# One product and a VectorE transpose for each squaring of a spectral-norm chain

## The chip, the cores and the metric

The kernel runs on one core of a Trainium2 chip. The metric is the device time of one execution in microseconds, the median of several runs.

## The reference

Four layers follow one another on x of shape (8, 512, 32, 32). Only the first is touched by the change.

```python
# layer 0
f_x = relu(batchnorm(conv1x1(x, Wf, bf), gamma_f, beta_f)).reshape(b, 64, hw)
g_x = relu(batchnorm(conv1x1(x, Wg, bg), gamma_g, beta_g)).reshape(b, 64, hw)
h_x = conv1x1(x, Wh, bh).reshape(b, 64, hw)
z = einsum('bcn,bcm->bnm', f_x, g_x)                 # hw x hw, rank 64
sigma = svd(z, compute_uv=False)[:, 0][:, None, None]
z2 = einsum('bnm,bcm->bcn', z / sigma, h_x).reshape(b, 64, h, w)
x = conv1x1(z2, Wv, bv) + x
# layer 1: group norm, attention over the 1024 positions, x + proj
# layer 2: attention with 128 channels, folded batch norm, + x
# layer 3: sign(x + bias) times sign(W), batch norm, + x, PReLU
```

## The kernel before

The images are in pairs, one on partitions 0-63 and one on 64-127. The largest singular value of an image comes from two 64x64 Gram matrices, F = f f' and G = g g': the largest eigenvalue of F G is sigma squared. `gram(j, i, ...)` makes them for pair j by TensorE and stores them, masked to the two diagonal 64x64 blocks (`mask2`, L1351), in `gm[j]`, 128x128 each: F at index 0, G at 1 and g h' at 2.

`chain(j, split)` then takes the product and squares it again and again. F G is not symmetric, and a product on TensorE takes its left operand transposed, so the chain keeps the matrix and its transpose: `products` makes both (L1029 and L1030, each 128 columns), and `evict` copies both from PSUM into `cur` (128 x 2 x 128). There are 21 products' steps in a chain: the first, then seven rounds (`NSTEP + 1`) of three squarings, the last round of two. In each third step the matrix is scaled by its trace: `diagonal` multiplies by the identity and sums each row (L1056), `total` sums the rows by a product with `mask2` (L1060) and copies the sum to `tr` (L1061), a reciprocal follows (L1083), and the eviction scales. These are the scaled steps, the others are plain. Logarithms of the traces give 1/sigma at the end, which scales g h' into index 0 of `gm[j]` (L1112), from where `weights0` (L290) takes it.

With `split`, in the head, the two products have banks of their own and VectorE and ScalarE evict one each. Without it both lie in one bank and one instruction evicts them: ScalarE in a plain step (L1043), VectorE in a scaled one (L1051).

The order of the work:
- The head. The first pair's chain (`jl`) runs alone, before any attention can start. TensorE's order there is the program's (`tc.manual_schedule`). Beside each step of the chain, `next(todo)` puts a piece of other work, a filler: 16 pieces of the weight product `wu` and of the first pair's last Gram, then 26 pieces of the other pairs' transposes, Grams and bias rows (L1142, L1342, L1313, L1315, L1420), then 16 of the weight product `wo` (L1288). A piece of a weight product is one product of 512 columns.
- `entering(0)`/`enter` of the first image follows, with the fillers left over between its steps. For each 512-column block it adds the layer's result to x (L421) and takes statistics (L424), then makes the group-norm means.
- The main part, one image after another in `fast`: seven-product matrix multiplications (`seven`, L388, whose results VectorE takes up at L345), attention values (L557), then layers 2 and 3. The other three pairs' chains are hidden there: `chore(2)` takes one step of `behind` for every second step of the image's own work. Outside the head the order on each engine is made by a scheduler from the dependencies.

The head's fillers before:

```python
for k, _ in enumerate(chain(jl, True)):
    for _ in range(4 if k == 3 * NSTEP + 3 else 2 if k % 3 == 1 or k == 0 else 1):
        next(todo, None)
...
for n in (2, 3, 3, 3, 4, 4, 6):
    next(steps)
    for _ in range(n):
        next(todo, None)
```

The functions that the diff touches, and what calls them:

Of the kernel before, what the change touches and what calls it, by code (L numbers as in the profile page):

```python
# [8 lines left out]
F32 = mybir.dt.float32  # L9
F16 = mybir.dt.float16  # L10
I32 = mybir.dt.int32
AF = mybir.ActivationFunctionType
ALU = mybir.AluOpType
# [3 lines left out]
P = 128  # L17
# [8 lines left out]
MID = 64  # L26
NPAIR = B // 2
# [42 lines left out]
NSTEP = 6  # L70
# [15 lines left out]
def kernel(  # L86
# [17 lines left out]
    nc = tc.nc  # L104
    mm = nc.tensor.matmul

    const = ctx.enter_context(tc.tile_pool(name="const", bufs=1))
    wpool = ctx.enter_context(tc.tile_pool(name="weights", bufs=1))
    keep = ctx.enter_context(tc.tile_pool(name="keep", bufs=1))
    xpool = ctx.enter_context(tc.tile_pool(name="x", bufs=2))  # L110
    stat = ctx.enter_context(tc.tile_pool(name="stat", bufs=2))
    spin = ctx.enter_context(tc.tile_pool(name="spin", bufs=2))
# [10 lines left out]
    def bank():  # L123
        return psum["bank"].tile([P, HF], F32, tag="bank", name="bank")
# [20 lines left out]
    def side(i):  # L145

        return slice(i * MID, (i + 1) * MID)
# [21 lines left out]
    ident = const.tile([P, P], F32, tag="ident", name="ident")  # L169
    make_identity(nc, ident)  # L170

    def block_ones(size, value, name):

        n = P // size
        member = const.tile([P, n], F32, tag=name + "_m", name=name + "_m")
        nc.vector.tensor_reduce(
            member, ident.rearrange("p (g j) -> p g j", j=size), AX.X, ALU.add
        )
        t = const.tile([P, n, size], F32, tag=name, name=name)
        nc.vector.tensor_scalar(  # L180
            t, member.unsqueeze(2).to_broadcast([P, n, size]), value, None, ALU.mult
        )
        return t.rearrange("p g j -> p (g j)")

    mask2 = block_ones(MID, 1.0, "mask2")
    gmat = block_ones(GROUP, 1.0 / GROUP, "gmat")

    fold = a1.tile([P, 2, MID], F32, tag="fold", name="fold")
# [13 lines left out]
    wv2 = const.tile([P, C], F32, tag="wv2", name="wv2")  # L202
# [40 lines left out]

    r_dram = [dram.tile([4, N // 4], F32, name=f"r_dram{i}") for i in range(2 * B)]
    f_dram = [dram.tile([P, HF], F32, name=f"f_dram{b}") for b in range(B)]
    gm = [keep.tile([P, 3, P], F32, tag=f"gm{j}", name=f"gm{j}") for j in range(NPAIR)]
    sw3 = wpool.tile([P, CC, C // 2], F16, tag="sw3", name="sw3")
    round3 = const.tile([P, 1], F32, tag="round3", name="round3")
    nc.gpsimd.memset(round3, ROUND)
# [36 lines left out]
    def weights0(b):  # L286

        rr = side(b % 2)
        ps = bank()
        mm(out=ps, lhsT=gm[b // 2][rr, 0, :], rhs=wv2[rr, :], start=True, stop=True)  # L290
        t = fpool.tile([P, C], F32, tag="pv", name="pv", bufs=2)
        if b % 2:
            nc.vector.tensor_copy(t, ps)
        else:
            nc.scalar.copy(t, ps)
        return t
# [716 lines left out]

        return hb, got[0] if more else None

    def chain(j, split):

        ff, gg, gh = (gm[j][:, i, :] for i in range(3))  # L1020
        tr = spin.tile([P, NSTEP + 3], F32, tag="tr", name="tr")

        def column(name):
            return spin.tile([P, 1], F32, tag=name, name=name)

        def products(a, at):
            ps = [bank()] if not split else [bank(), bank()]
            pa, pb = ps[0][:, 0:P], ps[-1][:, 0:P] if split else ps[0][:, P : 2 * P]
            mm(out=pa, lhsT=at, rhs=a, start=True, stop=True)  # L1029
            mm(out=pb, lhsT=a, rhs=at, start=True, stop=True)  # L1030
            return ps[0], pa, pb

        def evict(got, r=None, again=None, full=None):

            both, pa, pb = got
            cur = spin.tile([P, 2, P], F32, tag="cur", name="cur")
            parts = [(cur[:, 0], pa), (cur[:, 1], pb)]
            if not split:
                parts = [(cur.rearrange("p i c -> p (i c)"), both[:, 0 : 2 * P])]
            for i, (dst, ps) in enumerate(parts):  # L1040
                if r is None:
                    if i or not split:
                        nc.scalar.copy(dst, ps)  # L1043
                    else:
                        nc.vector.tensor_copy(dst, ps)
                elif i:
                    nc.scalar.activation(dst, ps, AF.Copy, scale=full)
                elif again is None:
                    nc.vector.tensor_scalar(dst, ps, r, None, ALU.mult)
                else:  # L1050
                    nc.vector.tensor_scalar(dst, ps, r, again, ALU.mult, ALU.mult)  # L1051
            return cur

        def diagonal(u, v, t):
            d = spin.tile([P, P], F32, tag="diag", name="diag", bufs=1)
            nc.vector.scalar_tensor_tensor(d, u, 1.0, v, ALU.mult, ALU.mult, accum_out=t)  # L1056

        def total(t, s, n=1):
            ps = bank()
            mm(out=ps[:, 0:n], lhsT=mask2, rhs=t, start=True, stop=True)  # L1060
            nc.vector.tensor_copy(tr[:, s : s + n], ps[:, 0:n])  # L1061

        t = column("tj")
        diagonal(ff, gg, t)
        got = products(gg, ff)
        total(t, 0)
        r = column("r")
        nc.vector.reciprocal(r, tr[:, 0:1])
        cur = evict(got, r, None, r)
        yield  # L1070

        root, half_ = column("root"), column("half_")
        nc.gpsimd.tensor_tensor(root, tr[:, 0:1], minus_half[:, 0:1], ALU.pow)
        nc.vector.tensor_tensor(half_, root, root, ALU.mult)
        nc.vector.tensor_tensor(half_, half_, tr[:, 0:1], ALU.mult)
        nc.vector.tensor_scalar(half_, half_, -0.5, 1.5, ALU.mult, ALU.add)
        nc.vector.tensor_tensor(root, root, half_, ALU.mult)
        for s in range(NSTEP + 1):
            got = products(cur[:, 0], cur[:, 1])
            if s:  # L1080
                total(t, s)
                r = column("r")
                nc.vector.reciprocal(r, tr[:, s : s + 1])  # L1083
                if split:
                    r2 = column("r2")
                    nc.vector.tensor_tensor(r2, r, r, ALU.mult)
                cur = evict(got, r, r, r2 if split else None)
            else:
                cur = evict(got)
            yield  # L1090
            for more in range(2 if s < NSTEP else 1):
                got = products(cur[:, 0], cur[:, 1])
                cur = evict(got)
                if more:
                    t = column("tj")
                    diagonal(got[1], ident, t)
                yield
        t = spin.tile([P, 2], F32, tag="td", name="td")
        diagonal(cur[:, 0], ident, t[:, 0:1])
        diagonal(cur[:, 0], cur[:, 1], t[:, 1:2])  # L1100
        total(t, NSTEP + 1, 2)

        ln = spin.tile([P, NSTEP + 2], F32, tag="ln", name="ln")
        rsig = column("rsig")
        nc.scalar.activation(ln, tr[:, 1:], AF.Ln)
        nc.vector.tensor_tensor(ln, ln, shares, ALU.mult)
        nc.vector.tensor_reduce(rsig, ln, AX.X, ALU.add)
        nc.scalar.activation(rsig, rsig, AF.Exp, scale=-0.5)
        nc.vector.tensor_tensor(rsig, rsig, root, ALU.mult)
        for i in range(2):  # L1110
            rr = side(i)
            nc.vector.tensor_scalar(  # L1112
                ff[rr, :].rearrange("p (i c) -> p i c", c=MID),
                gh[rr, rr].unsqueeze(1).to_broadcast([MID, 2, MID]),
                rsig[rr, :],
                None,
                ALU.mult,
            )
        ready.add(j)
        yield  # L1120

# [2 lines left out]

    def chains():
        for j in rest:
            yield from chain(j, False)

    behind = chains()
    env = {}  # L1130
# [208 lines left out]
    def gram(j, i, lt, rhs):  # L1339
        ps = wide()  # L1340
        for t in range(NT):
            mm(  # L1342
                out=ps[:, 0:P],
                lhsT=lt[:, t, :],
                rhs=rhs[:, t, :],
                start=t == 0,
                stop=t == NT - 1,
            )
            if t == NT // 2 - 1:
                yield  # L1350
        nc.vector.tensor_tensor(gm[j][:, i, :], ps[:, 0:P], mask2, ALU.mult)  # L1351
        yield

    def turned_pair(j):
# [28 lines left out]
    ps = bank()  # L1383
# [5 lines left out]
    ps = bank()  # L1389
# [64 lines left out]
    relus = iter([(2 * j + k, i) for j in rest for i in range(2) for k in range(2)])  # L1454
    with tc.manual_schedule(engines={mybir.EngineType.PE}):
        steps = entering(0)
        for k, _ in enumerate(chain(jl, True)):

            for _ in range(4 if k == 3 * NSTEP + 3 else 2 if k % 3 == 1 or k == 0 else 1):
                next(todo, None)  # L1460
            for args in (next(relus, None),):
                if args:
                    relu(*args)
        for n in (2, 3, 3, 3, 4, 4, 6):
            next(steps)
            for _ in range(n):
                next(todo, None)
        for _ in todo:
            pass
# [195 lines left out]
```

## Time and profile before

| | |
|---|---|
| median of 3 runs | 1898.42 us (1897.82 to 1898.85) |
| span of the profiled execution | 1896.9 us |
| TensorE busy | 1878.3 us (99%) |
| VectorE busy | 1097.5 us (58%) |
| ScalarE busy | 511.4 us (27%) |
| GpSimd busy | 225.7 us (12%) |
| mean granted TensorE clock | 0.998 |

The profiled execution's own time is its span, 1896.9 us from the first instruction to the last; the median of the runs lies 1.5 us above it. PE is TensorE's matmuls, PEld its weight loads, DVE is VectorE, ACT ScalarE, POOL GpSimd. L1029 is line 1029 of the kernel before. An f32 product shows as two instructions, one for each pass. The end of a matmul in the trace is modelled, so the cost of a product is read from one start to the next.

### The profile page before, as it was taken

Reading aid. Unit: us, or ns where it says so; the run is one execution under the profiler, and the core shown is the slowest. Engines: PE = TensorE matmul, PEld = TensorE weight load, DVE = VectorE, ACT = ScalarE, POOL = GpSimd, SP = SyncE. Lnnn points to the kernel's source line nnn. Section 1 sums busy time; section 2 is a strip of 40 time slices with the busy share of each in tenths; the row PEclk is TensorE's granted clock in tenths of the full one; section 3 lists DMA queues with packets and bytes.
Section 4 is the critical chain, followed back from the end, with each engine's and each line's share of the span. In section 5 each row is a group of like instructions: output and inputs, shape, how many; then the busy total and the mean of one; then the engine's idle time right before and its main releaser. Section 6 shows DMA issues by size and latency. Waiting matters only on the chain.

```text
span 1896.9 us, 16376 instructions
## 1 busy us (share of the span) xinstructions
PE 1878.3 (99%) x6178; PEld 976.1 (51%) x6178; DVE 1097.5 (58%) x1762; ACT 511.4 (27%) x811; POOL 225.7 (12%) x176
## 2 busy tenths in 40 slices
PE   9999999999999999999999999999999999999997
PEld 3366556544745446444645446544645455544653
DVE  3256576448664677338663675457753775466547
ACT  2142222034312432035202421144202521234013
POOL 0000111201121011200121001200130011101121
PEclk9999999999999999999999999999999999999999
DMA  8420000002000020002000110002000200000001
GB/s 314 168 78 6 1 6 12 1 12 89 17 1 0 34 72 12 1 12 89 18 0 0 42 65 12 0 23 78 12 1 12 89 12 0 1 34 22 12 0 47
DMA packets 25203, 66.52 MB, mean 35 GB/s; under 512 B 3552, under 2 KB 4764, under 8 KB 24476
## 3 DMA queue, kind: packets, MB, share of 16 engines
q1 hardware_dynamic: 24188, 64.96, 9.4%
q8 instruction: 51, 0.84, 0.2%
q10 hardware_dynamic: 864, 0.43, 0.1%
q14 instruction: 36, 0.29, 0.0%
q0 software_dynamic: 64, 0.00, 0.0%
HBM read 46.44 MB, written 18.94 MB: 34 GB/s over the span
## 4 chain that ended last, share of the span: by engine, by line
PE 98%; DVE 1%; ACT 0%; DMA 0%; issue 0%; POOL 0%; ACTq 0%; DVEq 0%
PE bank L388 46%; PE bank L557 20%; PE bank L958 6%; PE bank L806 6%; PE bank L1248 5%; PE bank L658 3%; PE bank L675 3%; PE bank L412 2%; PE bank L698 1%; PE wide L1288 1%; PE bank L1029 1%; PE wide L1342 1%; PE bank L1030 1%; PE quad L1142 1%; PE bank L829 0%; PE bank L1060 0%
## 5 line engine op out<-in xcount | busy, mean ns | idle before, releaser
L557 PE MATMUL bank<-e,vt 128*128 128x512 f32 x768 | 333.8, 592 | 0.0
L557 PEld LDWEIGHTS bank<-e,vt 128*128 128x128 f32 x768 | 145.0, 190 | 175.4 <-issue 173.4
L388 PE MATMUL bank<-ut,h 128*128 128x512 f32 x384 | 182.3, 597 | 0.0
L345 DVE TENSOR_TENSOR e<-bank,e 128x512 f32<-128x512 f32 x128 | 87.8, 686 | 81.0 <-PE bank L388 80.3
L388 PE MATMUL bank<-us,hs 128*128 128x512 f32 x256 | 121.5, 597 | 0.3 <-DVE us L317 0.3
L388 PEld LDWEIGHTS bank<-ut,h 128*128 128x128 f32 x384 | 71.4, 190 | 95.6 <-issue 84.5
L958 PE MATMUL bank<-e,tpg 128*128 128x512 f32 x256 | 114.7, 595 | 0.0
L806 PE MATMUL bank<-tpg 128*128 128x512 f32 x256 | 114.6, 592 | 0.0
L813 ACT ACTIVATE e<-bank 128x512 f32<-128x512 f32 x128 | 76.4, 597 | 128.5 <-PE bank L806 128.5
L360 POOL TENSOR_TENSOR e<-e 128x512 f32<-128x512 f32 x32 | 44.2, 1381 | 412.5 <-ACT e L339 144.1
L388 PE MATMUL bank<-wo,h 128*128 128x256 f32 x384 | 91.9, 382 | 0.0
L388 PE MATMUL bank<-h,wu 128*128 128x512 f32 x192 | 90.4, 593 | 0.1
L818 DVE TENSOR_TENSOR esum<-esum,e 128x1024 f32<-128x1024 f32 x48 | 58.8, 1225 | 54.5 <-ACT e L813 54.5
L345 DVE TENSOR_TENSOR vt<-bank,vt 128x512 f32<-128x512 f32 x64 | 44.1, 689 | 65.5 <-PE bank L388 64.7
L806 PEld LDWEIGHTS bank<-tpg 128*128 128x128 f32 x256 | 48.6, 190 | 60.7 <-issue 60.5
L958 PEld LDWEIGHTS bank<-e,tpg 128*128 128x128 f32 x256 | 48.1, 190 | 60.4 <-issue 60.3
L388 PEld LDWEIGHTS bank<-wo,h 128*128 128x128 f32 x384 | 71.6, 190 | 11.5 <-issue 2.5
L360 POOL TENSOR_TENSOR ut<-ut 128x512 f32<-128x512 f32 x16 | 21.8, 1365 | 465.3 <-ACT ut L341 465.3
L388 PEld LDWEIGHTS bank<-us,hs 128*128 128x128 f32 x256 | 47.1, 190 | 52.9 <-issue 47.8
L686 ACT ACTIVATE sg<-xt,rb 128x512 f16<-128x512 f32 x64 | 45.3, 718 | 100.7 <-DVE xt L677 97.1
L1248 PE MATMUL bank<-xt,fg 128*64 128x512 f32 x256 | 59.9, 616 | 4.4 <-DMA fg<-in_w_fg 4.4
L658 PEld LDWEIGHTS bank<-tpg,xt 128*128 128x128 f32 x512 | 59.5, 192 | 7.2 <-issue 7.2
(333 smaller groups left out, 2968.1 us busy)
## 6 DMA issues: line engine op xcount, KB each, us to landing
xt<-in_x SPq DMA_DIRECT2D x55, 512.0 KB
out<-both SPq DMA_DIRECT2D x63, 256.0 KB
rfull<-r_dram SPq DMA_DIRECT2D x15, 512.0 KB
f_dram<-f SPq DMA_DIRECT2D x8, 256.0 KB
fb<-f_dram SPq DMA_DIRECT2D x8, 256.0 KB
w<-in_w SPq DMA_DIRECT2D x1, 1024.0 KB
q<-in_w_q SPq DMA_DIRECT2D x1, 1024.0 KB
k<-in_w_k SPq DMA_DIRECT2D x1, 1024.0 KB
```

Of the source, the lines that this page charges most:

```text
L345: nc.vector.tensor_tensor(dst, ps, u, ALU.add)
L360: nc.gpsimd.tensor_tensor(c22, c22, c12, ALU.add)
L388: mm(out=ps[:, q * w : (q + 1) * w], lhsT=lt(ka, kb, q, k), rhs=rhs(ka, kb, q, k), start=first and q == 0 and k == 0, stop=last and k == 1 ...
L557: mm(out=ps, lhsT=a[:, t, bass.ts(r_, P)], rhs=e[t], start=first and t == 0, stop=last and t == NTH - 1, skip_group_check=True,)
L658: mm(out=ps[:, i, :], lhsT=xt[:, cc, bass.ts(4 * h + i, P)], rhs=sbw["tpg"][:, cc, 2 * P : 3 * P], start=cc == 0, stop=cc == CC - 1,)
L675: mm(out=ps, lhsT=sbw["z"][:, bass.ts(oc, P)], rhs=att, start=True, stop=True)
L686: nc.scalar.activation(sg[:, cc, :], xt[:, cc, half(h)], AF.Sign, bias=rb3[:, cc : cc + 1])
L806: mm(out=ps, lhsT=pt[:, 0, bass.ts(t, P)], rhs=tt[:, 0, half(h)], start=True, stop=True,)
L813: nc.scalar.activation(e[:, half(h)], ps, AF.Exp, scale=float(P) ** -0.5)
L818: nc.vector.tensor_tensor(esum, esum, e, ALU.add)
L958: mm(out=banks[h], lhsT=gt[:, t, :], rhs=es[t][:, half(h)], start=t == 0, stop=t == NT - 1,)
L1248: mm(out=banks[i][side(h), :], lhsT=w0[i][:, cc, :], rhs=xt[:, cc, half(h)], start=cc == 0, stop=cc == CC - 1,)
```

## The change

The chain keeps one matrix, 128 x 64 (the two images' 64x64 blocks one above the other), in `cur`, and its transpose as the block-diagonal 128x128 `ff`. A step is one product of 64 columns with `ff` stationary, one eviction, and six VectorE transposes that write the next `ff`: two instructions of 64x64[...] and four of 32x32 which put the off-diagonal blocks where they belong. All four chains do so. G and g h' are kept as 128x64 tiles (`gs_`, `gh_`), `eye2` takes the identity's place in the trace. In the head two fillers stand beside each step (four at the end), 46 in all instead of 33, and 12 instead of 25 are left for `enter`.

```diff
+    eye2 = const.tile([P, MID], F32, tag="eye2", name="eye2")
+    nc.vector.tensor_tensor(eye2, ident[:, 0:MID], ident[:, MID:P], ALU.add)
...
-    gm = [keep.tile([P, 3, P], F32, tag=f"gm{j}", name=f"gm{j}") for j in range(NPAIR)]
+    gm = [keep.tile([P, P], F32, tag=f"gm{j}", name=f"gm{j}") for j in range(NPAIR)]
+    gs_, gh_ = (
+        [keep.tile([P, MID], F32, tag=f"{n}{j}", name=f"{n}{j}") for j in range(NPAIR)]
+        for n in ("gg", "gh")
+    )
...
-        def products(a, at):
-            ps = [bank()] if not split else [bank(), bank()]
-            pa, pb = ps[0][:, 0:P], ps[-1][:, 0:P] if split else ps[0][:, P : 2 * P]
-            mm(out=pa, lhsT=at, rhs=a, start=True, stop=True)
-            mm(out=pb, lhsT=a, rhs=at, start=True, stop=True)
-            return ps[0], pa, pb
+        def product(a):
+            ps = bank()[:, 0:MID]
+            mm(out=ps, lhsT=ff, rhs=a, start=True, stop=True)
+            return ps
+
+        def turned(cur):
+            q = MID // 2
+            for i in range(2):
+                nc.vector.transpose(ff[side(i), side(i)], cur[side(i), :])
+            for i in range(2):
+                for k in range(2):
+                    to = slice(i * MID + k * q, i * MID + (k + 1) * q)
+                    of = slice(i * MID + (1 - k) * q, i * MID + (2 - k) * q)
+                    nc.vector.transpose(ff[to, of], cur[of, k * q : (k + 1) * q])
...
+        def evict(ps, r=None, again=None):
+            cur = spin.tile([P, MID], F32, tag="cur", name="cur")
+            if r is None:
+                nc.scalar.copy(cur, ps)
+            elif again is None:
+                nc.vector.tensor_scalar(cur, ps, r, None, ALU.mult)
+            else:
+                nc.vector.tensor_scalar(cur, ps, r, again, ALU.mult, ALU.mult)
+            turned(cur)
             return cur
...
-        nc.vector.tensor_tensor(gm[j][:, i, :], ps[:, 0:P], mask2, ALU.mult)
+        if i == 0:
+            nc.vector.tensor_tensor(gm[j], ps[:, 0:P], mask2, ALU.mult)
+        else:
+            for k in range(2):
+                nc.vector.tensor_copy((gs_, gh_)[i - 1][j][side(k), :], ps[side(k), side(k)])
...
-        for k, _ in enumerate(chain(jl, True)):
-            for _ in range(4 if k == 3 * NSTEP + 3 else 2 if k % 3 == 1 or k == 0 else 1):
+        for k, _ in enumerate(chain(jl)):
+            for _ in range(4 if k == 3 * NSTEP + 3 else 2):
                 next(todo, None)
...
-        for n in (2, 3, 3, 3, 4, 4, 6):
+        for n in (1, 1, 2, 2, 2, 2, 2):
             next(steps)
```

More of the change, by code (lines that the diff above doesn't have):

```diff
@@ L289, in weights0 @@
         ps = bank()
-        mm(out=ps, lhsT=gm[b // 2][rr, 0, :], rhs=wv2[rr, :], start=True, stop=True)
+        mm(out=ps, lhsT=gm[b // 2][rr, :], rhs=wv2[rr, :], start=True, stop=True)
         t = fpool.tile([P, C], F32, tag="pv", name="pv", bufs=2)
@@ L1014, in fast, with chain @@
         return hb, got[0] if more else None
-    def chain(j, split):
-        ff, gg, gh = (gm[j][:, i, :] for i in range(3))
+    def chain(j):
+        ff, gg, gh = gm[j], gs_[j], gh_[j]
         tr = spin.tile([P, NSTEP + 3], F32, tag="tr", name="tr")
@@ L1024, in column @@
             return spin.tile([P, 1], F32, tag=name, name=name)
-        def products(a, at):
-            ps = [bank()] if not split else [bank(), bank()]
-            pa, pb = ps[0][:, 0:P], ps[-1][:, 0:P] if split else ps[0][:, P : 2 * P]
-            mm(out=pa, lhsT=at, rhs=a, start=True, stop=True)
-            mm(out=pb, lhsT=a, rhs=at, start=True, stop=True)
-            return ps[0], pa, pb
[L1033 to L1051, printed above, removed]
@@ L1052, in evict @@
+        def evict(ps, r=None, again=None):
[7 more added lines that the diff above has]
+            turned(cur)
             return cur
         def diagonal(u, v, t):
-            d = spin.tile([P, P], F32, tag="diag", name="diag", bufs=1)
@@ L1056, in diagonal @@
-            nc.vector.scalar_tensor_tensor(d, u, 1.0, v, ALU.mult, ALU.mult, accum_out=t)
+            d = spin.tile([P, MID], F32, tag="diag", name="diag", bufs=1)
+            for i in range(2) if u is ff else [None]:
+                rr = slice(0, P) if i is None else side(i)
+                uu = u[rr, :] if i is None else u[rr, rr]
+                nc.vector.scalar_tensor_tensor(
+                    d[rr, :], uu, 1.0, v[rr, :], ALU.mult, ALU.mult, accum_out=t[rr, :]
+                )
         def total(t, s, n=1):
@@ L1064, in chain @@
         diagonal(ff, gg, t)
-        got = products(gg, ff)
+        got = product(gg)
         total(t, 0)
@@ L1068, in chain @@
         nc.vector.reciprocal(r, tr[:, 0:1])
-        cur = evict(got, r, None, r)
+        cur = evict(got, r)
         yield
@@ L1078, in chain @@
         for s in range(NSTEP + 1):
-            got = products(cur[:, 0], cur[:, 1])
+            got = product(cur)
             if s:
@@ L1083, in chain @@
                 nc.vector.reciprocal(r, tr[:, s : s + 1])
[L1084 to L1087, printed above, removed]
+                cur = evict(got, r, r)
             else:
@@ L1091, in chain @@
             for more in range(2 if s < NSTEP else 1):
-                got = products(cur[:, 0], cur[:, 1])
+                got = product(cur)
                 cur = evict(got)
@@ L1095, in chain @@
                     t = column("tj")
-                    diagonal(got[1], ident, t)
+                    diagonal(got, eye2, t)
                 yield
         t = spin.tile([P, 2], F32, tag="td", name="td")
-        diagonal(cur[:, 0], ident, t[:, 0:1])
-        diagonal(cur[:, 0], cur[:, 1], t[:, 1:2])
+        diagonal(cur, eye2, t[:, 0:1])
+        diagonal(ff, cur, t[:, 1:2])
         total(t, NSTEP + 1, 2)
@@ L1109, in chain @@
         nc.vector.tensor_tensor(rsig, rsig, root, ALU.mult)
[L1110 to L1118, printed above, removed]
+        nc.vector.tensor_scalar(
+            ff.rearrange("p (i c) -> p i c", c=MID),
+            gh.unsqueeze(1).to_broadcast([P, 2, MID]),
+            rsig,
+            None,
+            ALU.mult,
+        )
         ready.add(j)
@@ L1126, in chains @@
         for j in rest:
-            yield from chain(j, False)
+            yield from chain(j)
     behind = chains()
```

## The prediction

> **What bounds the kernel now.** I read the page first, for the engines and the chain of waits.
>
> ```profile
> PE 1878.3 (99%) x6178; PEld 976.1 (51%) x6178; DVE 1097.5 (58%) x1762; ACT 511.4 (27%) x811; POOL 225.7 (12%) x176
> ...
> PE 98%; DVE 1%; ACT 0%; DMA 0%; issue 0%; POOL 0%; ACTq 0%; DVEq 0%
> ```
>
> The second line is the chain that ended last, by engine. TensorE carries it nearly alone, so an instruction taken off TensorE shortens the kernel, unless TensorE then waits for something. What it could wait for is shown by the busy times in windows (columns: stretch, length, then busy us with counts for PE, PEld, DVE, ACT, POOL).
>
> ```profile
> 114.10:128.40 14.30, 14.25 (x61) 8.63 (x62) 4.91 (x26) 7.21 (x15) 0.55 (x1) 1.00 0.19 72
> 128.40:152.40 24.00, 22.82 (x180) 20.43 (x179) 18.46 (x55) 5.69 (x17) 0.00 (x0) 1.00 0.01 1
> ...
> 158.40:186.40 28.00, 28.00 (x129) 15.97 (x129) 18.72 (x47) 2.77 (x4) 1.02 (x1) 1.00 0.03 10
> 186.40:302.20 115.80, 115.40 (x425) 67.93 (x424) 75.53 (x161) 32.22 (x54) 13.28 (x11) 1.00 0.02 8
> ...
> 440.00:522.70 82.70, 82.70 (x322) 50.66 (x320) 56.85 (x123) 30.90 (x50) 9.78 (x8) 1.00 0.14 48
> ...
> 660.00:725.60 65.60, 65.60 (x231) 35.81 (x230) 48.27 (x91) 24.02 (x39) 6.84 (x5) 1.00 0.15 53
> ```
>
> The first two are the head's chain (products 0 to 8, then 8 to 20), the third is `enter` of the first image, the last three are where the hidden chains run most densely. TensorE is full everywhere. VectorE has 23% to 35% free in all but the first: that is the room for what the change puts on it.
>
> Next, what a product costs TensorE. The weight loads of one head step, in order of time (start, us, engine, line):
>
> ```profile
> 121.54 0.30 PEld L1029 LDWEIGHTS bank<-cur 128*128 128x128 f32 x2 [0.79 <-ACT cur L1043]
> 121.76 0.30 PEld L1030 LDWEIGHTS bank<-cur 128*128 128x128 f32 x2
> 121.98 0.30 PEld L1060 LDWEIGHTS bank<-tj,mask 128*128 128x128 f32 x2
> 122.21 0.30 PEld L1288 LDWEIGHTS wide<-nat_k,nat_q 128*128 128x128 f32 x2
> ```
>
> Each f32 product is two passes (x2). From start to start: 0.22 us for a product of 128 columns, 0.23 us for L1060, which streams one column. In the main part it is the same:
>
> ```profile
> 194.58 0.38 PE L1029 MATMUL bank<-cur 128*128 128x128 f32 x2
> 194.80 0.39 PE L1030 MATMUL bank<-cur 128*128 128x128 f32 x2
> 195.03 1.45 PE L388 MATMUL bank<-hs,su 128*128 128x512 f32 x3
> ```
>
> 0.45 us for the pair. So 64 columns instead of 128 save nothing; one product instead of two saves 0.225 us.
>
> Last, VectorE's instructions (source rows give min/median/max ns; the last three are from the timeline):
>
> ```profile
> L1112 DVE TENSOR_SCALAR gm<-gm,rsig x8: 270/283/288, 157.0 to 727.9; 64x128 f32<-64x128 f32 x8
> ...
> L1061 DVE COPY tr<-bank x32: 95/152/161, 115.0 to 723.3; 128x1 f32<-128x1 f32 x28, 128x2 f32<-128x2 f32 x4
> ```
>
> ```profile
> 120.53 0.29 DVE L1045 COPY cur<-bank 128x128 f32<-128x128 f32 x1 [1.01 <-PE bank L1029]
> 120.74 0.28 DVE L1056 SCALAR_TENSOR_TENSOR diag<-bank,ident 128x128 f32<-128x128 f32 x1
> ...
> 157.00 0.60 DVE L1112 TENSOR_SCALAR gm<-gm,rsig 64x128 f32<-64x128 f32 x2
> ```
>
> One column takes 152 ns, 128 columns some 285: about 0.15 us plus 1.04 ns a column. Two neighbours on the same partitions start 0.21 us apart, less than the duration (they overlap); the two of L1112, on partitions 0-63 and 64-127, take 0.60 us together, twice 0.28: no overlap.
>
> [...]
>
> **The change, part by part.**
>
> *TensorE.* 84 products go, one for each of 21 steps of 4 chains. Hidden chains: 63 x 0.225 = 14.2 us off a full TensorE. The head: 21 x 0.225 = 4.7 us.
>
> *The transposes.* Six a step, two of 64 columns and four of 32[...]. By the fit above 2 x 0.22 + 4 x 0.19 = 1.2 us in a row. [...] Lower bound: if they overlap as the 0.21 us pair does, 0.08 us less each, 0.75. I take 1.3, since L1112 shows no overlap. In all 84 x 1.3 = 109 us more of VectorE. It gives back little: the scaled evictions shrink from 0.54 (256 columns) to some 0.22 us, 21 times in the hidden chains, and in the head 14 copies (L1045) of 0.29 us go to ScalarE.
>
> *The head.* PE's order there is the program's, so what is late is waited for. Before, an eviction starts 0.43 us after its product and the next product follows at 1.25 to 1.5 us. After, a plain step is 0.45 (product to copy) + 0.25 (ScalarE) + 0.05 + 1.3 (transposes) + 0.15 = 2.2 us, against 0.22 + 2 x 0.86 = 1.94 us of TensorE's own. A scaled step (`total`, reciprocal, scaling ahead of the transposes) is 2.95 against 2.17. Then:
> - products 0 to 8: 3 x 2.95 + 5 x 2.2 = 19.9 us (14.9 before, with 12 fillers instead of 16);
> - products 8 to 20: the fillers are now nearly all the Grams and biases, whose VectorE work comes along: some 14.3 us (copies of 0.69, four sums of 0.68, eight bias rows of 0.48 to 0.75, mask and copies of `gram`), with 12 x 1.3 of transposes, 4 x 0.64 of totals and scalings, 4 x 0.38 of diagonals: 34 us for VectorE in a stretch whose TensorE work is 24. I take 36 (23.4 before);
> - the tail from product 20 to `weights0`: 6.5 (6.0 before);
> - `enter`: fillers fall from 25 to 12. Its own line is 0.5 + 0.6 + 0.5 for the first products and copies, 8 x 1.45 of VectorE (L421 and L424), some 5 for the means and 1 for the first normalized columns: 20 us (28.0 before).
>
> The sum is 82.4 against 72.3: **10 us lost**, the saving of 4.7 included. With transposes of 0.75 the plain step falls under TensorE's own time and the loss is about 3; with every hop late it is 14.
>
> *The hidden chains.* The stretch 186 to 302 has 24 of their steps, 440 to 523 has 15, 660 to 726 has 10. VectorE then: (75.5 - 3 + 31)/(115.8 - 5.4) = 94%, likewise 74.4/79.3 = 94% and 60/63.3 = 95%. Products stand 3.9 us apart there. A step's latency grows from about 1.5 us to 0.45 + 0.5 (ScalarE and its queue) + about 1 behind VectorE's 0.7 to 1.2 us operations + 1.3 = 3.3, more when scaled. A transpose also waits on ScalarE's copy at the head of VectorE's queue; behind it stand L345's evictions[...]. I charge 0.2 us for each of the 49 steps, **10 us**; bounds 1 (the cover holds, as between 426 and 446, where VectorE was full and TensorE never stopped) and 18. The other 14 steps, 7.4 us apart, cost nothing while that spacing holds; without it, 0.2 each.
>
> The rest: two half copies for each of the eight masked Grams not of index 0, `eye2` once, one final scaling instead of two: all under 0.5 us in sum, beside TensorE work except in the head, where it is in the 14.3. No DMA is added or moved.
>
> *Sum:* -14.2 + 10 + 10 = +6 us on 1896.9, the span profiled. The median of the runs is 1898.42, 1.5 us more for what lies around the span, so 1904.5.
>
> **The rivals.**
> - *The win survives (faster).* The transposes overlap, or VectorE's free third is enough: head +3, stalls 1, so -14.2 + 4 = -10: 1888. For it: TensorE full beside a full VectorE at 426 to 446. Against: L1112, and 94%. It decides if six transposes take under about 0.9 us. Chance 0.22.
> - *They cancel.* Head +8, stalls 6: 1898. Chance 0.16.
> - *VectorE becomes the bound in the dense stretches.* Head +14, stalls 18: 1916. Chance 0.15. Against: the load is under 100% on average.
> - *The change doesn't do what it says*, the second product being hidden anyway: excluded by the 0.45 us between L1029 and L388 on a full engine.
>
> The forecast itself has 0.47. Slower by over 0.2% (3.8 us, about what a measurement of this kernel can tell from no change): 0.62; within: 0.16; faster: 0.22. The range runs from the surviving win's 1888 to just above the VectorE-bound case, 1918; the likeliest case alone has 1901 to 1910.
>
> **What would show it.** Right: transposes of 190 to 260 ns, six in 1.2 to 1.4 us; L1029's successor once a step at 0.22 us; head (first product to the first L388) of some 82 us, with TensorE idle ahead of the products and VectorE over 90% from product 8 on; products in the main part waiting for a transpose. Wrong: a head of 75 or less, or an iteration 302 to 522 shortened by the full 22 x 0.225 = 5 us with no waits.

## The result and the profile after

The changed kernel takes 1928.26 us (median of 4 runs, 1922.33 to 1931.05), the kernel before, beside it on the same chip, 1898.12 us: a ratio of 1.0156, 95% interval 1.0144 to 1.0168. The forecast said slower, by 6 us; it is 30.

The profiled execution is the quickest of the four, 1922.33 us with a span of 1920.6, so its profile shows 24 of the 30 us. The other runs have a lower mean TensorE clock: 0.994 for a span of 1923.8, 0.992 for 1928.8 and 1929.2, against 0.996 here and 0.998 in every run of the kernel before. This second loss is taken up below.

The page after, with the engines' busy time and the chain that ended last:

```profile
PE 1870.6 (97%) x6010; PEld 958.2 (50%) x6010; DVE 1191.9 (62%) x2267; ACT 503.3 (26%) x804; POOL 225.2 (12%) x176
...
PE 85%; DVE 13%; issue 1%; ACT 1%; DMA 0%; POOL 0%; DVEq 0%; ACTq 0%
```

TensorE has 168 fewer instructions (84 products of two passes) and is busy 7.7 us less, VectorE 505 more instructions and 94 us more. What matters is the second line: VectorE's share of the chain was 1% and is 13%. The wait behind it, the largest of TensorE's list of waits (total us, times, longest):

```profile
PE bank L1032 <- DVE gm L1044: 23.9, 23, 3.3
```

L1032 is the one product that is left, L1044 the four 32x32 transposes. Eight of the waits, 9.1 us, are in the head, 15, 14.8 us, behind it. In the kernel before no wait for the chain reached 1 us; the largest is for the row sums:

```profile
PE bank L1060 <- DVE diag L1056: 0.4, 1, 0.4
```

The busy times in windows (stretch, length, busy us with counts for PE, PEld, DVE, ACT, POOL, then the granted TensorE clock, the DMA share, GB/s) for products 0 to 8, 8 to 20, the tail, `enter`, and two dense stretches of the hidden chains (the last at the same clock times as in the prediction, which is some 21 us earlier in the work):

```profile
113.30:135.20 21.90, 18.43 (x73) 9.81 (x73) 15.40 (x74) 5.79 (x12) 0.55 (x1) 1.00 0.11 42
135.20:172.00 36.80, 29.44 (x224) 27.39 (x224) 32.48 (x125) 5.10 (x14) 0.00 (x0) 0.95 0.00 1
172.00:178.80 6.80, 6.08 (x28) 3.75 (x28) 4.18 (x25) 3.19 (x5) 0.00 (x0) 1.00 0.00 1
178.80:199.80 21.00, 17.39 (x49) 6.02 (x49) 14.96 (x38) 2.61 (x3) 1.02 (x1) 1.00 0.05 13
200.70:326.00 125.30, 115.49 (x380) 63.72 (x379) 104.94 (x309) 29.49 (x54) 13.97 (x11) 0.99 0.02 7
440.00:522.70 82.70, 80.11 (x233) 37.41 (x232) 73.32 (x162) 33.20 (x54) 7.37 (x5) 1.00 0.15 54
```

TensorE stands still in each of them, and in two its clock is below 1.00. Where the 23.7 us between the spans are: the head (first product to first main product) takes 86.5 us after 72.6, **+13.9**; from there to the first attention value 123.2 after 115.3, **+7.9**; to the second image's 223.4 after 220.5, **+2.9**; to the third's 216.2 after 216.8, **-0.6**.

One plain step of the head, from the timeline (start, us):

```profile
117.41 0.21 ACT L1050 COPY cur<-bank 128x64 f32<-128x64 f32 x1 [1.81 <-PE bank L1032]
...
117.65 0.51 DVE L1039 STREAM_TRANSPOSE gm<-cur 64x64 f32<-64x64 f32 x2 [0.45 <-ACT cur L1050]
...
118.19 0.85 DVE L1044 STREAM_TRANSPOSE gm<-cur 32x32 f32<-32x32 f32 x4
...
119.19 0.41 PE L1032 MATMUL bank<-cur,gm 128*128 128x64 f32 x2
```

Its product began at 116.97, so the step is 2.22 us. The six transposes take 1.39 of it, one behind the other. Where VectorE has other work in its queue, it looks like this (VectorE between products 10, at 141.23, and 11, then TensorE's product 11):

```profile
143.40 0.68 DVE L1428 TENSOR_TENSOR su<-wu,su 128x512 f32<-128x512 f32 x1
144.00 0.15 DVE L1070 COPY tr<-bank 128x1 f32<-128x1 f32 x1
144.07 0.74 DVE L1319 SCALAR_TENSOR_TENSOR part<-nat_k,ct,part 128x512 f32<-128x512 f32 x1
144.73 0.15 DVE L1092 RECIPROCAL r<-tr 128x1 f32<-128x1 f32 x1
144.80 0.47 DVE L1317 TENSOR_SCALAR part<-p,bvc 128x512 f32<-128x512 f32 x1
145.18 0.34 DVE L1054 TENSOR_SCALAR cur<-bank,r 128x64 f32<-128x64 f32 x1
...
145.57 0.50 DVE L1039 STREAM_TRANSPOSE gm<-cur 64x64 f32<-64x64 f32 x2
146.10 0.85 DVE L1044 STREAM_TRANSPOSE gm<-cur 32x32 f32<-32x32 f32 x4
...
147.01 0.43 PE L1032 MATMUL bank<-cur,gm 128*128 128x64 f32 x2 [3.26 <-DVE gm L1044]
```

`total`, reciprocal and scaling each let one long filler (a sum of L1428, bias rows of L1319 and L1317) go ahead. The step took 5.8 us and TensorE stood still for 3.26.

### The profile page after: what moved, and what is told of

Read it like the earlier page. It is cut to its first block, busy times and chain, and to the rows that moved or that the text cites. A ratio compares the mean times of both kernels' runs of the same rounds, so it can differ in the third digit from the quotient of the medians.

```text
span 1920.6 us, 16510 instructions
## 1 busy us (share of the span) xinstructions
PE 1870.6 (97%) x6010; PEld 958.2 (50%) x6010; DVE 1191.9 (62%) x2267; ACT 503.3 (26%) x804; POOL 225.2 (12%) x176
## 4 chain that ended last, share of the span: by engine, by line
PE 85%; DVE 13%; issue 1%; ACT 1%; DMA 0%; POOL 0%; DVEq 0%; ACTq 0%
PE bank L394 38%; PE bank L563 19%; PE bank L964 6%; PE bank L812 6%; PE bank L1252 4%; PE bank L664 3%; PE bank L681 3%; DVE gm L1044 1%; PE bank L418 1%; PE bank L704 1%; DVE xt L427 1%; DVE st L430 1%; PE bank L1032 1%; DVE gm L1039 1%; DVE both L725 1%
## 5 line engine op out<-in xcount | busy, mean ns | idle before, releaser
L1044 DVE STREAM_TRANSPOSE gm<-cur 32x32 f32<-32x32 f32 x336 | 68.0, 202 | 6.0
```

What stands on the lines that cost most here:

```text
L1044: nc.vector.transpose(ff[to, of], cur[of, k * q : (k + 1) * q])
```

## The experiments

Theory A is the prediction's sum with the profile's sizes: the head and the hidden chains each lose by themselves, because a step now goes through VectorE. Rivals were that one of the two carries it all, that occupation of VectorE is enough, and that the clock is at the bottom of it (theory C). Every ratio is to the kernel before, run beside it; its medians lie between 1897.85 and 1898.22 us, so the runs can be compared with each other too.

**One half at a time.** `chain_old` is the chain of before, two products a step.

```diff
 # e1_hidden_only: hidden chains new, head and its fillers as before
-        for k, _ in enumerate(chain(jl)):
+        for k, _ in enumerate(chain_old(jl, True)):
 # e2_head_only: head and fillers new, hidden chains as before
-            yield from chain(j)
+            yield from chain_old(j, False)
```

e1_hidden_only, expected: 

> The three hidden chains as after, the head's chain and its fillers as before. Theory A (the two losses are independent: the head lost 14 us because its chain's steps became longer than its fillers, the main part lost 10 us net, 24 us of products waiting for transposes less 14 us of products saved): the head takes 72.6 us again, the main part keeps its loss, about 1908 us. Rival B (the main part's loss comes from the head, whose late finish leaves the first image's work bunched): the main part then gains its 14 us, about 1885 us.

Measured: 1908.66 us, ratio 1.0052 (1.0035 to 1.0069), clock 0.996 to 0.998. TensorE's waits, same view as above:

```profile
PE bank L1041 <- DVE gm L1053: 14.1, 14, 2.5
```

e2_head_only, expected: 

> The head's chain and its fillers as after, the three hidden chains as before. Theory A: the head takes about 86 us (first product to the first product of the main part) against 72.6, the main part is as before, about 1912 us, or 1914 with a stretch of half clock for TensorE behind the longest gap of the head (3.3 us ahead of product 11). Rival B: the head's loss brings more behind it, 1922 us or more.

Measured: 1914.72 us, ratio 1.0084 (1.0067 to 1.0101), clock 0.994 to 0.997. So both halves lose: the hidden chains 10 us, the head 17; together 27 of the 30. The head's 17 is more than the 13.9 of the windows. This profile's head takes 90.0 us, with the same code that took 86.5 in the change: three stretches of it, 3.4, 6.8 and 3.4 us, have a clock of 0.5, where the change's head has one of 3.4. So the head of this code is not one number: its length goes with the clock that it meets.

**The fillers as before**, the products new everywhere:

```diff
-            for _ in range(4 if k == 3 * NSTEP + 3 else 2):
+            for _ in range(4 if k == 3 * NSTEP + 3 else 2 if k % 3 == 1 or k == 0 else 1):
...
-        for n in (1, 1, 2, 2, 2, 2, 2):
+        for n in (2, 3, 3, 3, 4, 4, 6):
```

e3_old_fillers, expected: 

> After, with the fillers as before: one beside most steps of the head's chain, 25 left for the entry of the first image. Theory A (a step cannot be shorter than 2.2 us plain and 2.9 us scaled, and VectorE's filler work adds to that only where it is dense): products 0 to 20 take about 51 us instead of 58.7, the entry 28 instead of 21, the head as a whole 86 us, so about the same as after, 1922 to 1931. Rival C (moving the fillers is the loss, since it brings VectorE's work of 14 us into the chain): the head takes 78 us or less, 1915.

Measured: 1931.57 us, ratio 1.0187 (1.017 to 1.0205), clock 0.986 to 0.992. The head takes 95.5 us. Missed: products 0 to 20 take 57.8 us, not 51, and the head is 9 us longer than the change's, where I had expected about the same. With one filler beside a step TensorE waits for the transposes ahead of 17 products of the head instead of 8, and 24 us of this profile's head run at half clock, against 3.4. By the price of half clock that is worked out below, 0.3 to 0.5 us for each busy microsecond, that is 6 to 9 us, most or all of the 9: what the second filler of the change does is mainly to keep the clock up. In the medians it is worth 3 us.

**Occupation alone.** The kernel before, with six transposes of each hidden step's result that nobody reads:

```diff
+            if not split:
+                scrap = spin.tile([P, P], F32, tag="scrap", name="scrap", bufs=1)
+                ... the six transposes of the change, cur[:, 0, 0:MID] into scrap
             return cur
```

e4_dummy, expected: 

> The kernel before, with six VectorE transposes of the same shapes added to each step of the hidden chains; they write a scratch tile that nothing reads, so no product waits for them. 63 x 1.36 = 86 us more of VectorE. If VectorE's occupation is what stops TensorE in the main part, the loss is like after's 24 us of waits or at least half of it: 1910 to 1922. If it is the chain's longer latency (the next product waits for six transposes), the loss is small: 1898 to 1903.

Measured: 1909.01 us, ratio 1.0057 (1.0041 to 1.0074). Nothing is saved, no product depends on a transpose, and 11 us are lost, nearest to what was expected of occupation. VectorE is busy 1174.8 us, about as in e1 (1171.1). TensorE's waits:

```profile
PE bank L1071 <- DVE diag L1067: 7.1, 7, 2.4
...
PE bank L1029 <- DVE cur L1051: 1.1, 1, 1.1
```

They are for VectorE's own parts of the chain (row sums ahead of `total`, scaled evictions), now late behind the transposes. To compare it with e1 I took, in each stage, the stage's length less its matmul passes at their undisturbed spacing (0.43 us for 512 columns, 0.11 for up to 128), and the same for before; this is an estimate. Waits over those of before are 11.8 us in e4, 23.8 in e1 and 24.3 in the change. So VectorE's occupation by itself costs about half of what the hidden chains' waits cost; in it is also that VectorE stands still, 7.6 us in e4, until ScalarE's copies ahead of the transposes are done. It is a comparison of sizes and not a clean split: half of e4's waits, 5.9 us, come between the second and the third image's attention values, where e1 has 3.2; most of e1's come before.

**Steps taken out of the dense stretches.** Hidden chains new, head old, and no step beside the scores, where they stand 3.9 us apart; those steps fall later, beside the attention values, in the same or the next images.

```diff
 # e5_sparse
         for k, _ in enumerate(scores1(env, hb, ua, es)):
...
-            if not rest3 and k not in (13, 14, 15, 20, 21, 22):
-                chore(2)
 # e8_make_v: e5, and rarer steps beside V, from the second image on
         for k, _ in enumerate(make_v(hb, vt)):
...
-            chore(2)
+            chore(3 if n else 2)
```

e5_sparse, expected: 

> The hidden chains as after, the head's chain and fillers as before, and no chain steps beside the scores of the images (where products stood 3.9 us apart and VectorE was over 90% busy): they stand beside the making of u and v and the attention values alone. Theory A (the main part loses because the next product comes before the transposes are done): the waits shrink to 2 to 5 us and the products saved (63 x 0.225 to 0.275) show: 1884 to 1888. Rival (the transposes' mere occupation of VectorE, 86 us in all, costs the same wherever it stands, some 11 us as in the run with transposes that nothing reads): 1893 to 1897.

Measured: 1893.32 us (7 runs), ratio 0.9969 (0.9958 to 0.9981). The same products and transposes as in e1, 15 us quicker; waits by the same estimate 8.5 us instead of 23.8. It came out above the 1884 to 1888 that I gave if spacing was all, and at the edge of the rival's 1893 to 1897 (the occupation costs the same wherever it stands): some waits stay, and the steps beside V still stand closer than the others (3.7 us). The four runs with a clock of 0.997 take 1893.32 to 1893.54 us, the three at 0.998 1890.58 to 1891.41; the profile, at 0.997, has one stretch at half clock. So about 2.5 us of the median are the clock.

e8_make_v, expected: 

> As e5_sparse, and from the second image on a chain step only beside every third step of make_v (products 5.5 us apart instead of 3.7). Theory A (what is left of the waits, some 8 us by the time that the passes do not explain, stands where products are less than 4 us apart): two or so of it go, 1890 to 1892. Rival (what is left is VectorE's occupation, which is only moved): the same as e5_sparse, 1893.

Measured: **1889.63 us** (5 runs, 1889.12 to 1890.19), ratio 0.9954 (0.994 to 0.9967), its slowest run 7 us below the fastest of the kernel before. Of the 3.7 us that it is ahead of e5 most is the clock, which is 0.998 or 0.999 here in every run, without half clock in the profile ahead of the last 10 us; against e5's runs at 0.998 it is 1.3 us. Its page and TensorE's waits:

```profile
PE 1865.5 (99%) x6052; PEld 962.5 (51%) x6052; DVE 1168.4 (62%) x2156; ACT 506.2 (27%) x811; POOL 219.9 (12%) x176
```

```profile
PE bank L1039 <- DVE gm L1051: 2.4, 4, 0.8
```

VectorE is as busy as in e1 (1168.4 us after 1171.1), but TensorE waits for the chain's transposes four times, 2.4 us in all, instead of 14 times and 14.1. By the estimate above some 5 us of waits are left, against 11.8 in e4 with the same load, so the occupation does not cost the same wherever it stands. What decides in these runs is not how much VectorE does but where.

**Shorter transposes by a stacked tile.** The transposed matrix kept as 128x64 instead of block-diagonal, so that one 128x64 transpose does for the two of 64x64, and two products on 64 rows and 64 columns of the array do for one.

```diff
-            mm(out=ps, lhsT=ff, rhs=a, start=True, stop=True)
+            for i in range(2):
+                mm(out=ps[side(i), :], lhsT=ff[side(i), :], rhs=a[side(i), :], start=True, stop=True)
...
-            for i in range(2):
-                nc.vector.transpose(ff[side(i), side(i)], cur[side(i), :])
+            nc.vector.transpose(ff, cur)
```

e9_stacked_sparse (on e8), expected: 

> As e8_make_v, with the transpose kept as 128 x 64 like the matrix itself instead of block-diagonal: one VectorE instruction of 128x64 in place of the two of 64x64 (0.24 instead of 0.51 us), and two products of 64x64 side by side in place of one of 128x128. 63 x 0.27 = 17 us less of VectorE, the latency of a step 0.27 us less, TensorE the same or up to 0.1 us less a step. Theory A: 1 to 3 us less waiting and 0 to 6 us less of TensorE, 1884 to 1890. Rival (the waits left have another cause): within 1 us of e8_make_v.

Measured: 1901.83 us (16 runs), ratio 1.0019 (1.0012 to 1.0027): 12 us slower than e8 (11.2 us between the spans profiled), where both theories had it level or better (the up to 0.1 us less of TensorE a step was a guess without a measurement). The timelines show where. In e8 (PE, then PEld):

```profile
763.35 1.02 PE L572 MATMUL bank<-e,vt 128*128 128x512 f32 x2
764.21 0.33 PE L1039 MATMUL bank<-cur,gm 128*128 128x64 f32 x2
764.38 1.08 PE L572 MATMUL bank<-e,vt 128*128 128x512 f32 x2
```

```profile
763.78 0.19 PEld L1039 LDWEIGHTS bank<-cur,gm 128*128 128x128 f32 x1 [0.24 <-DVE xd L342]
764.21 0.19 PEld L1039 LDWEIGHTS bank<-cur,gm 128*128 128x128 f32 x1 [0.24 <-issue]
```

and in e9:

```profile
748.19 1.02 PE L572 MATMUL bank<-scratch 128*128 128x512 f32 x2
749.14 0.33 PE L1040 MATMUL bank<-cur,gm 64*64 64x64 f32 x4
749.40 0.70 PE L572 MATMUL bank<-e,vt 128*128 128x512 f32 x1
```

```profile
749.14 0.20 PEld L1040 LDWEIGHTS bank<-cur,gm 64*64 64x64 f32 x4 [0.76 <-issue]
```

In e8 the first weights are loaded at 763.78, 0.43 us ahead of their product, while the product in front still runs; in e9 the 64x64 load begins only with its own product, at 749.14. The two passes in front take 0.95 us instead of 0.86, and the chain's product holds TensorE 0.26 us instead of 0.17; the pass behind takes 0.05 us longer than in e8 too. Together it is 0.24 us a step, as the spacing of the steps beside the attention values shows, 7.33 us after 7.09. 63 times that is 15 us, 4 more than the spans differ: by this sum the shorter transposes gave some 4 us of waiting back, and TensorE's waits for the transposes fall from 2.4 to 0.2 us. Why the 64x64 weights come no earlier was not shown, nor how much of the 0.24 us is their late load.

e10_stacked (on the change), expected: 

> After with the transpose kept as 128 x 64 in all four chains, head's too, so a step's transposes take 1.1 instead of 1.36 us. Theory A (each 0.27 us of transposes is on the path of the head's 21 steps, and the hidden steps wait less): head 80 to 82 us instead of 86.5, the main part's waits 19 instead of 24 us, 1914 to 1921. Rival (the head is set by the fillers' VectorE work and the clock rather than by the transposes): head above 84, 1923 or more.

Measured: 1923.0 us, ratio 1.0129 (1.0114 to 1.0145), clock 0.995 in all runs; the profile's span is 1921.2, the change's 1920.6, and the head takes 86.7 us, as before this edit. By these numbers the rival is right, but they hide two gains. In the head a plain step has gone from 2.22 to 2.18 only: the transposes end 0.24 us sooner, but TensorE's own two fillers and the dearer product now end last. Products 0 to 8 still take 1 us less (20.8 after 21.9). Behind them this profile has 13.7 us at half clock, where the change's has 3.4, by the price below 3 to 4.5 us more. In the main part TensorE waits for the transposes 7 times, 3.5 us, where the change has 15 times and 14.8, and the dearer products, 63 times 0.24 us, take that back. The median is 5 us under the change's, with the spans profiled equal; the change's other runs have the lower clock, which suggests that the 5 us are the clock.

**The clock.** Two attempts to keep TensorE busy in the changed head: three unread products beside each step from the 8th on (e6), and the pieces of `wo` ahead of the Grams and biases, so that VectorE's long fillers come later (e7).

```diff
 # e6_warm
+            spare = bank() if k > 6 else None
+            for _ in range(3 if k > 6 else 0):
+                mm(out=spare[:, 0:P], lhsT=ident, rhs=ident, start=True, stop=True)
 # e7_quiet_fillers
+        yield from product(nat["v"], sbw["p"], wo, False)
         between = biases()
...
-        yield from product(nat["v"], sbw["p"], wo, False)
```

e6_warm, expected: 

> After, with three products of 128 columns into a bank that nothing reads, behind the fillers of each step of the head's chain from the eighth on (14 x 0.67 = 9.4 us of TensorE work, into a stretch with some 13 us of TensorE idle). Theory C (the spread of after's runs, 1922 to 1931, is the stretches of half clock behind the gaps of the head): no half clock in the head's chain, runs within 3 us of each other, 1921 to 1926. Rival (the clock is not what spreads them, or the gaps are not what lowers it): the same spread and clocks of 0.992 to 0.996, and 1928 to 1936 for the added work.

Measured: 1928.55 us, ratio 1.0165 (1.015 to 1.0181), head 89.9. Theory C's 1921 to 1926 without half clock did not come, but the theory was not put to the test: the unread products run before the wait of product 11 and the gap stays (TensorE idle for 2.7 of the 4 us from 144 to 148), with a stretch of 3.4 us at half clock behind it as in the change.

e7_quiet_fillers, expected: 

> After, with the 16 pieces of the weight product wo (which bring VectorE no work) put ahead of the Grams and bias rows among the fillers, so that products 8 to 16 of the head's chain stand beside them and 12 of the pieces with VectorE work stand beside the entry of the first image. Theory A (VectorE's load sets products 8 to 20): these steps shorten to 2.2 us plain and 2.9 scaled, products 8 to 20 take some 32 us instead of 36.9, the gap of 3.3 us is gone, and the entry grows by 3 to 6 us: head 84 to 88. Rival (the chain's own latency alone sets it): products 8 to 20 stay at 36 or more.

Measured: 1927.55 us, ratio 1.0159 (1.0143 to 1.0174), head 91.9. Products 8 to 20 fall from 36.8 to 34.6 us, between the two expectations, and what was put off then comes in the tail and `enter`: the tail runs with a gap of its own (1.7 us) and 10.2 us at half clock behind it. The head is 5.4 us longer than the change's, of which its extra half clock is 3 to 4.5 by the price below. Put elsewhere in the head, the same VectorE work cost no less.

So the clock was tested by itself, in the kernel before, with unread copies of a product ahead of its eviction:

```diff
+            late[0] += 1
+            for _ in range({11: 14}.get(late[0] - 1, 0) if split else 0):   # e12: {9: 7, 13: 7}
+                scrap = spin.tile([P, P], F32, tag="scrap", name="scrap", bufs=1)
+                nc.vector.tensor_copy(scrap, pa)
```

e11_one_gap, expected: 

> The kernel before, with 14 unread copies of the product (128 columns each, from PSUM) by VectorE ahead of the eviction of the head's product 11, so that TensorE stands still once for some 2.5 to 3.5 us. Theory C (a gap of about 3 us in the head makes TensorE's clock fall to half for a stretch of 3.4 us behind it, which costs some 1.5 us more than the gap): 1902.5 to 1904, granted clock 0.997, and the windows behind the gap show a clock of 0.5. Rival (the low clock of the changed kernel has nothing to do with its gaps): the gap alone, 1900.5 to 1902, clock 0.998 and no half clock.

Measured: 1907.14 us, ratio 1.0051 (1.0034 to 1.0067), clock 0.996.

e12_two_gaps, expected: 

> The kernel before, with the same 14 copies in two places, seven ahead of the eviction of product 9 and seven ahead of that of product 13: two gaps of about 1 us. Theory C: no half clock, each gap costs itself alone: 1899.5 to 1900.5, clock 0.998. Rival (any idle time of TensorE lowers the clock in proportion): as much over the gaps' own time as in the kernel with one gap.

Measured: 1908.36 us, ratio 1.0056 (1.0039 to 1.0073), clock 0.995 to 0.997. Both expectations had the gaps too small: in VectorE's order a filler stands after nearly every copy, and the gaps are 8.8 us in e11, 4.3 and 3.5 us in e12. So e12 does not show whether gaps of 1 us leave the clock alone, but that gaps of 3.5 to 8.8 us bring half clock is plain. The kernel before has its clock at 1.00 throughout the head; with gaps put into it, half clock follows each: 10.2 us in e11, from inside the gap on, and 3.4 us behind each gap of e12. Windows of e12, cut at the edges of its half-clock stretches and in steps of their length:

```profile
132.94:136.36 3.42, 0.30 (x3) 0.33 (x4) 3.11 (x11) 0.00 (x0) 0.00 (x0) 1.00 0.00 0
136.36:139.77 3.41, 3.41 (x19) 3.41 (x18) 1.09 (x5) 0.37 (x1) 0.00 (x0) 0.50 0.00 0
...
146.60:150.01 3.41, 0.01 (x1) 0.00 (x0) 3.41 (x12) 0.00 (x0) 0.00 (x0) 1.00 0.01 2
150.01:153.42 3.41, 3.29 (x15) 3.32 (x16) 0.93 (x2) 0.27 (x1) 0.00 (x0) 0.50 0.00 0
```

A window in which TensorE was nearly idle (busy for 0.30 and 0.01 us) is followed by one at half clock, though TensorE is full again (3.41 and 3.29). The two stretches begin 13.65 us apart, four times 3.41; in the profiles of the change, e2, e3 and e7 too, the stretches of one run begin whole multiples of 3.41 us apart (46; 2 and 14; 7 and 12; 8). So in each of these profiles they lie on one grid of 3.41 us. The changed kernel, cut 0.2 and 0.3 us beside the edges:

```profile
144.79:148.20 3.41, 1.19 (x10) 1.20 (x11) 3.23 (x15) 0.21 (x1) 0.00 (x0) 0.98 0.00 0
148.20:151.61 3.41, 3.41 (x19) 3.41 (x19) 2.85 (x11) 0.21 (x1) 0.00 (x0) 0.52 0.00 0
...
301.95:305.40 3.45, 0.99 (x7) 0.80 (x5) 3.21 (x10) 0.00 (x0) 0.00 (x0) 0.95 0.01 4
305.40:308.80 3.40, 3.37 (x10) 2.86 (x11) 2.59 (x12) 0.21 (x1) 1.02 (x1) 0.55 0.43 160
```

The first pair is the 3.26 us gap ahead of product 11. What a stretch costs is an estimate: half of what TensorE is busy in it, 1.7 of 3.41 us, if at a clock of 0.50 everything takes twice as long. The same work in the head keeps TensorE busy for 71.0 us before, 72.1 in e11 with 3.4 busy us at half clock and 73.9 in e12 with 6.7: 0.3 to 0.4 us for each, and e2's head against the change's gives 0.4. So I take 0.3 to 0.5, and the two stretches are 2 to 3.4 of this profile's 24 us.

## Why the prediction was right and wrong

**Right, by its own steps.** Products: the steps beside the attention values come 7.31 us apart before and 7.09 after, 0.22 for the product gone. Transposes: 240 and 203 ns (190 to 260), six in 1.39 us (1.2 by the fit, 1.3 taken, the 0.1 more without a measurement; 1.2 to 1.4 given), one behind the other like L1112's two in the kernel before (0.60 us for twice 0.28). The plain step: 2.22 us for 2.2. Products 8 to 20: 36.8 for 36, with VectorE at 32.5 for 34, 88% of the stretch where over 90% was named; this is in part luck, since a stretch at half clock that no term had lies in it. The tail is 6.8 for 6.5, `enter` 21.0 for 20. The cover that was named for the steps 7.4 us apart holds but for one wait of 2.22 us in the change's profile (before, between 426 and 446, TensorE was busy for all of the 20 us beside VectorE's 19.79): e5 and e8 gain by using it.

**First mis-sized term, the hidden chains: 10 us charged, about 24 measured**, beyond the bound of 18. This is the step that failed most. I charged 0.2 us for each of 49 dense steps. By the estimate above it was 24.3/49, 0.5 us, if all is put on them. The 94% were right as a demand, but I read them as a room of 6% that only now and then lets a wait through. e4 shows that the occupation alone costs some 12 us, with no product waiting for a transpose; that the latency of the step costs the other 12 is the difference, and not measured by itself. Both terms belonged in the sum, and I had put a number on their mixture. The window afterwards shows VectorE at 104.94 of 125.3 us, 84%: it reads as lower than forecast, because TensorE's waiting has stretched the stage.

**Second, the head: 10 charged, 13.9 measured.** About half of the difference, 2.0 us, is in products 0 to 8, 21.9 instead of 19.9, and there in the scaled steps. I gave each 2.95 us, as if nothing stood in VectorE's queue. They took 3.7, 2.8 and 4.2: in the last, the copy of `wu` (1.22 us) comes between `total` and its reading, and a sum of 0.68 between that and the reciprocal. A scaled step has four hops through VectorE's queue, not one, and each can meet a long filler. Of products 8 to 20, 1 to 1.7 us is half clock.

**Third, a term that was not there: the clock.** No step of the prediction asked what a gap in TensorE does to TensorE. In the profile it is 2 to 3.4 us, inside the two terms above. In the other three runs it is probably what makes the 3.2 to 8.6 us of span that they have over the profiled one: a mean clock lower by 0.004 is, as an estimate, 15 us more at half speed, or 4.6 to 7.7 us at 0.3 to 0.5 for each if TensorE is busy in them, and the runs at 0.992 are 8.2 and 8.6 us longer. Runs of other kernels go the same way: in e2 the two at 0.994 are 4.2 us longer than the two at 0.997, in e5 the four at 0.997 2.5 us longer than the three at 0.998. That gaps cause half clock is shown (e11, e12); that these runs had more of it is read from their mean clock alone, since they have no profile. Why one execution has more than another was not shown. That the grid of 3.41 us falls differently on the same gaps is a guess; the heads of the change and of e2, one code with 3.4 and 13.7 us at half clock, fit it.

The sum with the measured sizes: -14 + 24.3 + 13.9 = +24 us, the 23.7 of the spans, and some 6 more in the median. Of the rivals, "VectorE becomes the bound" came nearest (head +14, stalls 18, 1916); I had argued against it that the load is under 100% on average. None of the cases had the clock, and none had the hidden waits above 18.

## What to carry to other kernels

Work that moves from a full engine to one with a third of its time free cost next to nothing here only where the steps were far enough apart (2.4 us of waits for the transposes in e8, 14.1 in e1). Count the hops that the step makes through the other engine's queue, and charge one long neighbour to each, and charge the occupation separately. Here the same edit of the hidden chains is a loss of 10 us with most steps 3.9 us apart and a gain of 8.5 us with most of them 5.5 to 7 us apart, so try first where the steps are sparse. Where TensorE is the bound, a gap in it can have a second price, the half clock behind it (here in stretches of 3.41 us, each 1.0 to 1.7 us by the estimate above), and two kernels are compared fairly only when the stretches at half clock in their profiles are counted too.

## What the hardware showed that I had not expected

- The clock falls after less idleness than theory C had it, a gap of about 3 us: in e11 it fell from 1.00 to 0.50 at 137.46, 1.9 us after TensorE stopped. The profiles of the change, e2, e3, e7, e11 and e12 were cut into windows of 3.41 us on the grid of each, from the head's chain to some 760 us; the clock falls 13 times there. Every full-clock window in which TensorE was busy for at most 1.37 us, six of them, was followed by half clock. Of 11 with 1.40 to 1.88 us, 5 were. It is no exact rule: two falls came behind fuller windows (2.3 and 3.3).
- Two products on 64x64 tiles cost TensorE 0.24 us a step more than one on 128x128 with half its weights zero (e9 against e8). In the step shown their weights are not loaded ahead (749.14, with the product, against 0.43 us before it in e8); whether that is all of the cost is not shown.
